# Two PSUM banks in turn, a convolution in six steps and column sums with standing ones, in a kernel of selective scans

## The chip, the cores and the metric

The kernel runs on one core of one Trainium2 chip. The metric is the device time of one execution in microseconds (us). All runs here are of state "fast" (one core, no second state seen). Engines are named as in the profile: PE is TensorE, PEld its weight loads, DVE VectorE, ACT ScalarE, POOL GpSimd, SP the engine that issues the DMAs. `L401` is a line of the kernel; one helper issues most VectorE and GpSimd instructions, so they are told apart by their tiles. A "step" below is a `yield` in a Python generator: the kernel is built by several generators that are advanced in turn, once per scan ("piece"), so a step decides beside which scan an instruction stands in its engine's queue. In the changed kernel's trace all 3198 instructions of VectorE, 5567 of ScalarE and 2255 of GpSimd run in the order of the built program, so an instruction that waits holds up all that stand behind it on its engine.

## The reference, cut to what matters

```python
# per image (4 of them): x is 64 x 64 x 96
xz = bilinear(gn(x), W_in, ...)                    # two halves: xc, z (192 channels each)
t = conv3x3(sign(xc + move0), sign-weights) + conv_b + rp_b0
t = where(t >= 0, t, prelu_a * t) + rp_b1 + xc     # the PReLU
u = silu(t)                                        # written by rows and by columns
# 4 directions: u by rows, by columns, and both reversed
delta = softplus(dts + dt_bias)                    # dts, B, C from a projection of sign(u)
for l in range(4096):                              # the selective scan, 192 channels x 16 states
    h = exp(delta[l] * A) * h + (delta[l] * u[l]) * B[l]
    y[l] = sum over states of h * C[l]
# sum of the 4 directions, layernorm, gate, projection; then attention and a feed-forward layer
```

## The kernel before

It cuts the scans into 1536 pieces of 128 x 1024 (8 channels x 16 states on the partitions). Each piece needs: the decay dA on ScalarE (1.12 us), the input product on GpSimd (2.36 us), the scan on VectorE (2.34 us), the output product on VectorE (1.225 us) or GpSimd (2.35 us), and the sum over states on TensorE. Every eight pieces ScalarE copies the sums `y` out of their PSUM bank, and the delta of a later group is prepared. Everything else (column sums, convolution, projection, epilogue) is "side work", one step per piece.

```python
# the loop, cut
for i in range(n):
    ...
    if i >= 1: self.carry(i - 1)                   # ScalarE, 128x1
    if i % 8 == 3 and i > 8: self.evacuate(i - 4)  # ScalarE copies y out
    if i + 1 < n: self.decay(i + 1)                # ScalarE, dA of the next scan
    if i >= 3: self.reduce(i - 3)                  # TensorE, y in the bank "y"
    if i + AHEAD < n: self.inject(i + AHEAD)       # GpSimd, input product
    self.scan(i)                                   # VectorE
    c.later.tick()                                 # stores that are due
    if i % 8 == 0 and self.todo: lanes.append(self.prepare())
    interleave(lanes); next(back, None)            # one step of delta, one of the side work

# prepare(): delta, its bank is "dps"
<8 matmuls into ps>;                     yield
ACT Abs -> d; ACT Relu -> t;             yield
ACT Exp d; ACT Ln -> ps;                 yield
<TensorE adds t into ps by the identity>; yield
DVE d[:, 1] = ps * u;                    yield     # the product reads ps
ACT d[:, 0] = copy of ps                           # so does the copy

# convolution, for each 96 x 512 part: four steps of 5, 4, 5, 4 taps, and for the part before it
#   step 0: DVE pz = pz*s + v;  DVE pz = r*(1 - a) + pz
#   step 1: ACT sign(pz), ACT Exp    step 2: ACT Ln, Exp    step 3: DVE u = pz*e, ACT turned copy of u
# then a fifth step: ACT v, r from the bank, matmul into pz
```

## Time and profile before

| | before |
|---|---|
| median of the first three runs (5533.6 to 5543.78) | 5537.85 us |
| VectorE busy, of the profiled span of 5538.9 us | 5052.4 us (91%) |
| GpSimd busy | 4994.2 us (90%) |
| ScalarE busy | 3556.7 us (64%) |
| TensorE busy | 3432.7 us (62%) |

The prediction shows the main lines. Three more lines of the list of waits (waiting instruction, what it waited for, total us, times, longest us) turn out to matter:

```profile
ACT ut L614 <- DVE u L401: 91.6, 45, 3.6
...
DVE u L401 <- ACT e L601: 39.8, 16, 2.5
...
ACT pd L1185 <- DVE pd L401: 3.7, 1, 3.7
```

ScalarE's turned copy of u waits 91.6 us for VectorE's u, which stands in the same step. ScalarE's copy of delta (pd), which stands one step behind VectorE's product on the same bank, hardly waits at all: 3.7 us, once. VectorE waits for its inputs of u only in the first convolution, before the scans (16 times).

### The profile page before, as it was taken

What the parts mean: (1) busy time and instruction counts of PE and PEld (TensorE: products, weight loads), DVE (VectorE), ACT (ScalarE), POOL (GpSimd) and SP (SyncE); (2) the same over time, 40 slices, a digit from 0 to 9 for tenths busy, and PEclk for the clock granted to TensorE, in tenths of its full rate; (3) what the DMA queues carried; (4) which work ended last, traced back from release to release, by engine and by line L of the source; (5) the groups of instructions that cost most, each with busy time, mean ns of one, the idle gap of its engine ahead of it and who ended that gap; (6) DMA issues with size and microseconds to landing.
All of it is one profiled execution on the core that took longest, in us unless ns stands there. A gap on an engine that the chain in (4) does not pass through costs nothing. (4 is left out here: it accounts for less than half of the span.)

```text
span 5538.9 us, 62371 instructions
## 1 busy us (share of the span) xinstructions
PE 3432.7 (62%) x20197; PEld 1356.7 (24%) x20197; DVE 5052.4 (91%) x3237; ACT 3556.7 (64%) x5564; POOL 4994.2 (90%) x2262
## 2 busy tenths in 40 slices
PE   6456665576557766577656766544676564444677
PEld 3222222222223222222222222211232121111223
DVE  3299999999999999899999999999999999999984
ACT  4467776777666667677766666755556775555554
POOL 2199999999999999899999999999999999999981
PEclk8667776678767876667777777766787766566778
DMA  4456666866766566666656566665666665665652
GB/s 78 118 179 198 207 194 193 258 193 199 220 203 194 194 205 199 218 217 207 205 193 212 185 200 210 212 211 191 210 215 186 191 205 198 205 208 190 207 159 60
DMA packets 613244, 1069.93 MB, mean 193 GB/s; under 512 B 225083, under 2 KB 343924, under 8 KB 611124
## 3 DMA queue, kind: packets, MB, share of 16 engines
q1 hardware_dynamic: 599428, 1065.88, 61.4%
q8 instruction: 159, 2.61, 0.2%
q10 hardware_dynamic: 13488, 0.07, 0.1%
q14 instruction: 169, 1.38, 0.1%
HBM read 833.20 MB, written 229.38 MB: 192 GB/s over the span
## 5 line engine op out<-in xcount | busy, mean ns | idle before, releaser
L401 POOL TENSOR_TENSOR w<-dl,bc 128x1024 f32<-128x1024 f32 x1536 | 3579.9, 2356 | 166.7 <-PE yp L1302 93.2
L1231 ACT ACTIVATE dA<-dl,anm 128x1024 f32<-128x1024 f32 x1536 | 1715.6, 1117 | 477.0 <-DVE w L401 291.5
L1302 PE MATMUL yp<-w,sum 128*32 128x256 f32 x12288 | 1261.6, 507 | 1083.2 <-ACT ys L1316 621.9
L401 DVE TENSOR_TENSOR_SCAN dA<-dA,cy,w 128x1024 f32<-128x1024 f32 x706 | 1654.4, 2343 | 94.7 <-ACT dA L1231 83.4
L401 POOL TENSOR_TENSOR w<-h,bc 128x1024 f32<-128x1024 f32 x596 | 1402.6, 2353 | 93.7 <-DVE h L401 85.2
L401 DVE TENSOR_TENSOR w<-dA,bc 128x1024 f32<-128x1024 f32 x940 | 1151.4, 1225 | 47.7 <-DVE dA L401 0.5
L401 DVE TENSOR_TENSOR_SCAN h<-dA,cy,w 128x1024 f32<-128x1024 f32 x446 | 1043.3, 2340 | 9.2 <-ACT dA L1231 8.7
L1302 PEld LDWEIGHTS yp<-w,sum 128*32 128x32 f32 x12288 | 308.0, 127 | 2136.9 <-issue 705.4
L1271 ACT COPY cy<-dA 128x1 f32<-128x1 f32 x707 | 110.8, 157 | 692.0 <-DVE w L401 690.7
L401 DVE TENSOR_TENSOR_SCAN dA<-dA,w 128x1024 f32<-128x1024 f32 x234 | 534.2, 2283 | 22.3 <-ACT dA L1231 18.0
L577 PE MATMUL cv<-tp,cw 96*96 96x512 fp8e5 x1152 | 359.9, 456 | 85.6 <-ACT r L627 70.5
L401 DVE TENSOR_TENSOR_SCAN h<-dA,w 128x1024 f32<-128x1024 f32 x150 | 341.8, 2279 | 24.4 <-POOL w L401 23.6
L1179 PE MATMUL dps<-sp,ident 128*128 128x512 f32 x378 | 356.8, 1043 | 0.0
L1307 PE MATMUL yp<-ya,back 128*128 128x256 f32 x576 | 237.8, 534 | 0.0
L577 PEld LDWEIGHTS <-cw 96*96 96x96 fp8e5 x1152 | 159.0, 146 | 277.5 <-issue 223.8
L1271 ACT COPY cy<-h 128x1 f32<-128x1 f32 x445 | 82.7, 186 | 145.6 <-DVE h L401 144.5
L847 PE MATMUL yc<-eys,mean 96*96 96x512 f32 x240 | 134.6, 713 | 33.3 <-DMA eys<-yd 14.5
L1307 PEld LDWEIGHTS yp<-ya,back 128*128 128x128 f32 x576 | 123.9, 248 | 127.8 <-issue 97.1
L1172 ACT ACTIVATE pd<-dps,dbias,pvd 128x512 f32<-128x512 f32 x189 | 143.8, 761 | 16.4 <-PE dps L1167 13.0
L1173 ACT ACTIVATE sp<-dps,dbias,pvd 128x512 f32<-128x512 f32 x189 | 144.7, 766 | 0.0
L401 DVE TENSOR_TENSOR pd<-dps,pu 128x512 f32<-128x512 f32 x189 | 127.6, 675 | 4.6 <-DMA dl<-dld 4.3
L1316 ACT COPY ys<-yp 128x512 f32<-128x512 f32 x192 | 111.7, 582 | 30.2 <-PE yp L1307 24.3
(282 smaller groups left out, 4017.6 us busy)
## 6 DMA issues: line engine op xcount, KB each, us to landing
dl<-dld SPq DMA_DIRECT2D x768, 512.0 KB
bc<-bcd SPq DMA_DIRECT2D x512, 512.0 KB
dld<-pd SPq DMA_DIRECT2D x126, 512.0 KB
yd<-ys SPq DMA_DIRECT2D x768, 64.0 KB
dld<-pd SPq DMA_DIRECT2D x126, 256.0 KB
ya<-yd SPq DMA_DIRECT2D x192, 128.0 KB
pu<-ud SPq DMA_DIRECT2D x32, 512.0 KB
pu<-utd SPq DMA_DIRECT2D x31, 512.0 KB
```

The lines of the kernel that those rows point to most:

```text
L401: return getattr(self.eng, name)(out, *args, **kw)
L577: nc.tensor.matmul(ps, c.cw[:, j, t, 96 * h : 96 * h + 96], tpad[j][:, 8 * q + dy : 8 * q + dy + 8, dx : dx + IW], start=(j == 0 and t == ...
L847: self.c.nc.tensor.matmul(ps, w, x, start=(i == 0), stop=(i == len(pairs) - 1))
L1172: nc.scalar.activation(d[:, 0], ps, AF.Abs, scale=sc, bias=bi)
L1173: nc.scalar.activation(t, ps, AF.Relu, scale=sc, bias=bi)
L1179: nc.tensor.matmul(ps, c.ident, t, start=False, stop=True, skip_group_check=True)
L1231: c.nc.scalar.activation(t, self.dlt[i // NQ][0], AF.Exp, scale=c.anm[:, g, NQ * KORD[e] + q : NQ * KORD[e] + q + 1])
L1271: self.c.nc.scalar.copy(self.carries[g, q], h[:, CH - 1 : CH])
L1302: c.nc.tensor.matmul(y[32 * x : 32 * x + 32, g % 2, :], c.sum4, prod[:, 256 * x : 256 * x + 256], start=(q == 0), stop=(q == NQ - 1 and no ...
L1307: c.nc.tensor.matmul(y[:, g % 2, :], w, src, start=False, stop=(n == len(more) - 1))
L1316: c.nc.scalar.copy(t, y[:, :, ::-1] if k >= 2 else y)
```

## The change

Its intent: TensorE should no longer wait 622 us for the copy of `y` (two banks in turn); VectorE should be relieved of 48 steps of 0.75 us (TensorE adds the relu term in the bank); the side work's steps should be smaller; the column sums should take fewer passes of TensorE.

```diff
-        ps = ... tile(..., tag="dps")              # delta's bank
+        ps = ... tile(..., tag=f"y{1 - self.bank()}")
-            self.ydone[i // 8] = ... tag="y"
+            self.ydone[i // 8] = ... tag=f"y{i // 8 % 2}"
         nc.scalar.activation(d[:, 0], ps, AF.Abs, scale=sc, bias=bi)
+        yield
         nc.scalar.activation(t, ps, AF.Relu, scale=sc, bias=bi)
         yield
         nc.scalar.activation(d[:, 0], d[:, 0], AF.Exp, scale=-1.0)
+        yield
         nc.scalar.activation(ps, d[:, 0], AF.Ln, bias=1.0)
 ...
         c.vec.tensor_tensor(d[:, 1]..., ps..., uv, ALU.mult)
-        yield
         nc.scalar.copy(d[:, 0], ps)
 ...
+            if i + 1 < n:
+                self.decay(i + 1)
             if i % 8 == 3 and i > 8:
                 self.evacuate(i - 4)
-            if i + 1 < n:
-                self.decay(i + 1)
-            if i % 8 == 0 and self.todo:
+            if i % 8 == 4 and self.todo:           # and a fourth delta before the first scan
 # convolution (batches 1 to 3; the first keeps the old steps)
-                for s in range(4):                 # 5, 4, 5, 4 taps
+                for s in range(4 if alone else 5): # 4, 4, 4, 4, 2 taps
+                    if s == 0 and turned:
+                        by_columns(*turned)        # turned copy of the u before, and its store
-                            c.vec.scalar_tensor_tensor(pz, r, c.oma[:, one(ph)], pz, ALU.mult, ALU.add)
+                        elif s == 1 and not alone:
+                            nc.tensor.matmul(pz, c.omad[:, ph], r, start=False, stop=True, ...)
+                        elif s == (3 if alone else 4):
+                            if not alone:
+                                sign(ph, pq, pz)   # before: beside the first Exp
                             u = f32("u" + pn)[0:96]
                             c.vec.tensor_tensor(u, pz, e, ALU.mult)
+            if turned:
+                by_columns(*turned)                # the last one: after the last step
             c.later.flush()
             sub.close()
 # column sums: ones stand, x streams
-            for i in range(NT):
-                nc.tensor.matmul(csum, xts[i // 8][:, i % 8, :], c.ones1, ...)
+            for i in range(0, NT, 4):
+                nc.tensor.matmul(csum, c.ones1, xts[i // 8][:, i % 8 : i % 8 + 4, :]..., ...)
+            # then a copy of the row of 384, four tiny matmuls that turn and add it, a copy
```

(Cut; the scans' carry tiles are also joined, four to a tile.)

More of the change, by code (lines that the diff above doesn't have):

```diff
@@ L137, in hybrid_kernel @@
     acs, acb, oma = ctile("acs", [96, 2]), ctile("acb", [96, 2]), ctile("oma", [96, 2])
+    omad = ctile("omad", [96, 2, 96])
     sbR = ctile("sbR", [128, 2, 2])
@@ L188, in transposed @@
             count[0] += 1
-            ps = p.ps.tile([128, 1024], BF16, name=f"tps{count[0]}", tag=("y", "dps")[count[0] % 2])
+            ps = p.ps.tile([128, 1024], BF16, name=f"tps{count[0]}", tag=f"y{count[0] % 2}")
             at = 0
@@ L277, in weights @@
         nc.vector.tensor_scalar(oma, pv[:, :, PRELU], -1.0, 1.0, ALU.mult, ALU.add)
+        for h in range(2):
+            nc.gpsimd.tensor_scalar(omad[:, h], i96, oma[:, h : h + 1], None, ALU.mult)
         yield
@@ L350, in weights @@
         )
-        ps = p.ps.tile([128, 512], F32, name="tpd", tag="dps")
+        ps = p.ps.tile([128, 512], F32, name="tpd", tag="y0")
         for g in range(3):
@@ L507, in prologue @@
                 yield
-            csum = bank("csum", 0)[0:96, 0:1]
-            for i in range(NT):
-                nc.tensor.matmul(csum, xts[i // 8][:, i % 8, :], c.ones1, start=(i == 0), stop=(i == NT - 1))
-                if i % 8 == 7:
-                    yield
+            csum = bank("csum", 0)[0:1, 0 : 4 * DM]
+            for i in range(0, NT, 4):
+                nc.tensor.matmul(
+                    csum, c.ones1, xts[i // 8][:, i % 8 : i % 8 + 4, :].rearrange("p i e -> p (i e)"),
+                    start=(i == 0), stop=(i == NT - 4),
+                )
+                if i % 8 == 4:
+                    yield
+            row = f32("csr")[0:1, 0 : 4 * DM]
+            nc.scalar.copy(row, csum)
+            ps = bank("cst", 1)[0:96, 0:1]
+            for i in range(4):
+                nc.tensor.matmul(
+                    ps, row[:, DM * i : DM * i + DM], c.ones1[0:1, :], start=(i == 0), stop=(i == 3)
+                )
+            yield
             cs = f32("cs")[0:96, 0:1]
-            nc.scalar.copy(cs, csum)
-            gsum = bank("gsum", 1)[0:96, 0:1]
+            nc.scalar.copy(cs, ps)
+            gsum = bank("gsum", 0)[0:96, 0:1]
             nc.tensor.matmul(gsum, c.grp, cs, start=True, stop=True)
@@ L563, in prologue, with by_columns, sign @@
             one = lambda h: slice(h, h + 1)
-            prev = None
+            prev = turned = None
             two = c.p.dA.tile([128, CH], F32, name=f"cv2_{b}", tag="dA") if alone else None
             utp = sub.enter_context(tc.tile_pool(name=f"ut_{b}", bufs=1))
+            uts = {}
+            def by_columns(h, q, u):
+                if q % 4 == 0:
+                    uts[h] = utp.tile([96, IW, 32], F32, name=f"ut{h}{q}_{b}", tag="ut")
+                ut, at = uts[h], 8 * (q % 4)
+                dst, src = ut[:, :, at : at + 8], u.rearrange("p (h w) -> p w h", w=IW)
+                (nc.gpsimd.tensor_copy if alone else nc.scalar.copy)(dst, src)
+                if q % 4 == 3:
+                    rows = slice(8 * q - 24, 8 * q + 8)
+                    c.later.store(c.utd[b][h].rearrange("p (w h) -> p w h", h=IH)[:, :, rows], ut, after=1)
+            def sign(h, q, pz):
+                sg = f32(f"sg{h}{q}")[0:96, 0:128]
+                nc.scalar.activation(
+                    sg.bitcast(F8).rearrange("p (h e i) -> p h e i", h=8, e=2),
+                    pz.rearrange("p (h i e) -> p h e i", h=8, e=2), AF.Sign, saturate=False,
+                )
+                for m in range(3):
+                    g0 = 64 * (m // 2) + 32 * h
+                    c.later.store(xgw[g0 : g0 + 32, m % 2, 128 * q : 128 * q + 128], sg[m::3, :])
             for n, part in enumerate(parts + [None]):
@@ L572, in prologue @@
                     ps = (two[:, at : at + 512] if alone else bank("cv" + nm, 0))[0:96]
-                for s in range(4):
+                for s in range(4 if alone else 5):
                     if part:
-                        for j, t in taps[(0, 5, 9, 14)[s] : (5, 9, 14, 18)[s]]:
+                        per = 5 if alone else 4
+                        for j, t in taps[per * s : min(18, per * s + per)]:
                             dy, dx = divmod(t, 3)
@@ L581, in prologue @@
                             )
+                    if s == 0 and turned:
+                        by_columns(*turned)
+                        turned = None
                     if prev:
@@ L585, in prologue @@
                             c.vec.scalar_tensor_tensor(pz, pz, pv[:, ph, S_X : S_X + 1], v, ALU.mult, ALU.add)
-                            c.vec.scalar_tensor_tensor(pz, r, c.oma[:, one(ph)], pz, ALU.mult, ALU.add)
-                        elif s == 1:
-                            sg = f32("sg" + pn)[0:96, 0:128]
-                            nc.scalar.activation(
-                                sg.bitcast(F8).rearrange("p (h e i) -> p h e i", h=8, e=2),
-                                pz.rearrange("p (h i e) -> p h e i", h=8, e=2), AF.Sign, saturate=False,
-                            )
-                            for m in range(3):
-                                g0 = 64 * (m // 2) + 32 * ph
-                                c.later.store(xgw[g0 : g0 + 32, m % 2, 128 * pq : 128 * pq + 128], sg[m::3, :])
+                            if alone:
+                                c.vec.scalar_tensor_tensor(pz, r, c.oma[:, one(ph)], pz, ALU.mult, ALU.add)
+                        elif s == 1 and not alone:
+                            nc.tensor.matmul(pz, c.omad[:, ph], r, start=False, stop=True, skip_group_check=True)
+                        elif s == (1 if alone else 2):
+                            if alone:
+                                sign(ph, pq, pz)
                             e = f32("e" + pn)[0:96]
                             nc.scalar.activation(e, pz, AF.Exp, scale=-1.0)
-                        elif s == 2:
+                        elif s == (2 if alone else 3):
                             nc.scalar.activation(e, e, AF.Ln, bias=1.0)
                             nc.scalar.activation(e, e, AF.Exp, scale=-1.0)
-                        else:
+                        elif s == (3 if alone else 4):
+                            if not alone:
+                                sign(ph, pq, pz)
                             u = f32("u" + pn)[0:96]
@@ L605, in prologue @@
                             c.later.store(c.ud[b][ph][:, 512 * pq : 512 * pq + 512], u)
-                            if pq % 4 == 0:
-                                ut = utp.tile([96, IW, 32], F32, name=f"ut{pn}_{b}", tag="ut")
-                            at = 8 * (pq % 4)
-                            dst, src = ut[:, :, at : at + 8], u.rearrange("p (h w) -> p w h", w=IW)
+                            turned = (ph, pq, u)
                             if alone:
-                                nc.gpsimd.tensor_copy(dst, src)
-                            else:
-                                nc.scalar.copy(dst, src)
-                            if pq % 4 == 3:
-                                rows = slice(8 * pq - 24, 8 * pq + 8)
-                                c.later.store(
-                                    c.utd[b][ph].rearrange("p (w h) -> p w h", h=IH)[:, :, rows], ut, after=1
-                                )
+                                by_columns(*turned)
+                                turned = None
                     yield
@@ L633, in prologue @@
                     yield
+            if turned:
+                by_columns(*turned)
             c.later.flush()
@@ L1113, in __init__ @@
         self.bt, self.ct, self.dlt, self.ins, self.dAs, self.carries, self.ydone = {}, {}, {}, {}, {}, {}, {}
-        self.late = None
+        self.late, self.cys = None, {}
         self.us, self.gs, self.at, self.loaded, self.sums = {}, {}, -1, set(), {}
@@ L1119, in done, with bank @@
         return self.at > (b * NK + n) * NPC + SETTLE
+    def bank(self):
+        return max(0, self.at - 3) // 8 % 2
     def load_signs(self, b, k):
@@ L1161, in prepare @@
         d = spare[0] if spare else p.pd.tile([128, 2, 512], F32, name=f"pd_{nm}", tag="pd")
-        ps = spare[3] if spare else p.ps.tile([128, 512], F32, name=f"dps_{nm}", tag="dps")
+        ps = spare[3] if spare else p.ps.tile([128, 512], F32, name=f"dps_{nm}", tag=f"y{1 - self.bank()}")
         pv = ps.rearrange("p (c q s) -> p s q c", q=4, s=8)
@@ L1175, in prepare @@
         nc.scalar.activation(d[:, 0], d[:, 0], AF.Exp, scale=-1.0)
+        yield
         nc.scalar.activation(ps, d[:, 0], AF.Ln, bias=1.0)
@@ L1189, in prepare @@
             then = (lambda: self.loaded.add((b, k, ci, part))) if x == len(groups) - 1 else None
-            c.later.store(dst, d[r0 : r0 + n], after=1, then=then)
+            c.later.store(dst, d[r0 : r0 + n], after=2, then=then)
     def load_bc(self, w, to, b, e, ci, q):
@@ L1246, in scan @@
         if ci < NCH - 1:
-            self.carries[g, q] = c.p.cy.tile([128, 1], F32, name=f"cy_{i}", tag=f"cy{g}{q}")
+            if q == 0:
+                self.cys[g] = c.p.cy.tile([128, NQ], F32, name=f"cy_{i}", tag=f"cy{g}")
+            self.carries[g, q] = self.cys[g][:, q : q + 1]
         lead = c.vec.us - c.gps.us
@@ L1297, in reduce @@
         if i % 8 == 0:
-            self.ydone[i // 8] = c.p.ps.tile([128, 2, 256], F32, name=f"yp_{i}", tag="y")
+            self.ydone[i // 8] = c.p.ps.tile([128, 2, 256], F32, name=f"yp_{i}", tag=f"y{i // 8 % 2}")
         y, prod = self.ydone[i // 8], self.ins.pop(i)
@@ L1324, in run @@
         c, lanes, n = self.c, [], len(self.pieces)
-        w = [c.p.w.tile([128, CH], F32, name=f"w_s{x}", tag="w") for x in range(7)]
+        w = [c.p.w.tile([128, CH], F32, name=f"w_s{x}", tag="w") for x in range(8)]
         ps = [c.p.dA.tile([128, CH], F32, name=f"dA_s{x}", tag="dA") for x in range(2)]
@@ L1345, in run @@
             self.load_dl(m)
+        u = c.p.pu.tile([128, CH], F32, name="pu_s", tag="pu")
+        for _ in self.prepare((w[7].rearrange("p (t l) -> p t l", t=2), w[4][:, 512:CH], u, ps[1][:, 512:CH])):
+            pass
         self.decay(0)
```

## The prediction

> **What bounds the kernel now.** The time before is 5537.85 us. I read the page's busy table first, then the costliest groups, then who waited for whom on VectorE and GpSimd, then the engines' busy time in stretches that I cut at the stages of the side work.
>
> ```profile
> span 5538.9 us, 62371 instructions
> PE 3432.7 (62%) x20197; PEld 1356.7 (24%) x20197; DVE 5052.4 (91%) x3237; ACT 3556.7 (64%) x5564; POOL 4994.2 (90%) x2262
> L401 POOL TENSOR_TENSOR w<-dl,bc 128x1024 f32<-128x1024 f32 x1536 | 3579.9, 2356 | 166.7 <-PE yp L1302 93.2
> L401 POOL TENSOR_TENSOR w<-h,bc 128x1024 f32<-128x1024 f32 x596 | 1402.6, 2353 | 93.7 <-DVE h L401 85.2
> L401 DVE TENSOR_TENSOR w<-dA,bc 128x1024 f32<-128x1024 f32 x940 | 1151.4, 1225 | 47.7 <-DVE dA L401 0.5
> ```
>
> VectorE and GpSimd are both over 90% busy over the whole span. Each of the 1536 scans needs an input product on GpSimd, and afterwards an output product on VectorE (940 of them, 1.225 us) or GpSimd (596, 2.353 us). A counter in the kernel, at build time, deals out the output products, so the two engines form one balanced bound. The stretches (columns: length, then busy us of PE, weight loads, DVE, ACT, POOL; then the TensorE clock) show where they are not full:
>
> ```profile
> 0.00:269.00 269.00, 151.29 (x745) 87.85 (x746) 75.59 (x137) 121.16 (x198) 42.28 (x104) 0.79 0.44 95
> 771.00:961.00 190.00, 109.47 (x888) 48.62 (x886) 181.05 (x104) 127.81 (x195) 182.20 (x80) 0.65 0.61 191
> 1157.00:1429.00 272.00, 186.19 (x1084) 73.61 (x1083) 266.68 (x180) 198.13 (x303) 267.14 (x116) 0.79 0.69 207
> 1638.00:2270.00 632.00, 442.11 (x2320) 162.95 (x2320) 606.39 (x381) 423.81 (x678) 606.07 (x266) 0.73 0.61 196
> 4580.00:4804.00 224.00, 102.22 (x693) 34.21 (x692) 221.22 (x127) 116.93 (x172) 220.45 (x96) 0.61 0.60 195
> 5419.00:5539.00 120.00, 82.76 (x292) 36.68 (x284) 53.42 (x97) 52.31 (x88) 6.95 (x7) 0.79 0.22 62
> ```
>
> First and last are the start (before the first scan) and the end (after the last): 389 us that the change hardly touches. The stretch from 4580 has no side work: 71 scans in 224 us, 3.16 us each, VectorE 98.8% busy. That is the floor. The stretch from 1157 is a convolution: 79 scans, 3.44 us each, yet VectorE is still 98% busy. So a convolution costs time because it gives VectorE **work**, not because it makes it wait. The projection of B and C (from 771) and the epilogue (from 1638) lose 4 to 5% as **waits**.
>
> ```profile
> DVE dA L401 <- ACT dA L1231: 101.3, 86, 5.5
> DVE h L401 <- POOL w L401: 23.6, 2, 14.4
> DVE g L401 <- PE sy L847: 19.7, 9, 4.6
> POOL w L401 <- PE yp L1302: 93.6, 58, 8.6
> POOL w L401 <- DVE h L401: 85.2, 107, 4.1
> PE yp L1302 <- ACT ys L1316: 621.9, 141, 10.8
> ```
>
> (Total us, times, longest.) TensorE waits 622 us for ScalarE's copy of y out of its only bank: the change aims at this. But VectorE waits for GpSimd's products only twice, at the start, while GpSimd waits 85 us for scans. So VectorE leads; TensorE's wait costs time only if it delays GpSimd further than its lead, or holds ScalarE so that the next decay (dA) comes late. I followed each VectorE wait on ScalarE's dA (or its carry copy) over 0.2 us in the loop, some 119 us, back on ScalarE: about 45 us (39 waits near 1.25 us) stand behind a decay that itself waited for VectorE; 27 us behind the epilogue's squares waiting for the yc matmuls; 7 us behind the column sum; 6 us behind turned y still being loaded; and only 4 to 5 us behind the copy of y.
>
> **What the Trainium skill says.** "TensorE: Matmul & The Clock Gate", section "What's actually happening": TensorE drops to half rate after an idle window of about 3.4 us. The trace agrees: eight y matmuls take 1.08 us after a wait of 10 us for the copy and 0.64 us in a busy stretch. Shorter TensorE waits may so speed up what follows. "PSUM — Partial Sum Buffer", section "The four PSUM rules": a matmul without the first-flag adds to what VectorE wrote where the bit stands. Hence the new relu matmul must wait for VectorE's remaining step in that bank; the kernel before already adds the delta's relu term in this way. "DVE: opcode table, instruction layouts, handler registers and perf-mode slots", section "6. Datapath and trigger behaviour": the scan runs at half throughput. The trace agrees (2.34 us against 1.225 us for a product of the same size), so VectorE's main load stays.
>
> **The change, part by part.** I compared the order of instructions of both builds.
> *Relu term on TensorE.* VectorE loses 48 of its 64 scalar-tensor-tensor steps cz<-r,oma,cz (batches 1 to 3; the first keeps its 16) at 751 ns: 36.0 us. The counter then moves 9 output products from GpSimd to VectorE: +9 x 1.225 = 11.0 us. Net VectorE -25.0 us, GpSimd -9 x 2.353 = -21.2 us. Both lie on the bound in stretches 98% busy, so I take the mean: **-23 us**. TensorE gains 48 matmuls of two passes (its f32 counts are twice the instructions), at about 713 ns a pass (the yc row of the same shape): 68 us over three convolutions of some 275 us, where it is 64 to 72% busy. That fits beside the rest.
> *Six steps instead of five.* Four taps a step instead of five, ScalarE's copy of u moved away from u itself. ScalarE's 92 us of waiting for u should vanish, but the convolution's VectorE idles only 5 us in each, so: 0 to -2 us. The side work gets 48 steps longer; in both orders it finishes in time for the fourth direction, without a burst of catch-up.
> *Two banks in turn.* y of one group of eight pieces in one bank, the delta of the next in the other, then swapped. Delta's matmuls begin at piece 4 of a group and ScalarE's last copy of it is issued at piece 10, just before y of the next group wants that bank at piece 11. So TensorE no longer waits for the copy of y, issued at piece 11, but for the copy of delta at piece 10: about one scan (3.4 us) earlier, minus the decay ahead of it. I expect the 622 us to fall to some 300 to 400 us under a new name, not to zero. What of this reaches VectorE: the 4 to 5 us above, with the decay now ahead of the copy of y, and perhaps a fifth of the epilogue's 27 us through a warmer, less late TensorE: **-10 us**.
> *Column sums.* Before: 64 passes a batch, four steps of about 2.7 us. After: 8 matmuls of 384 columns, 16 passes, by the same 713 ns x 384/512 = 535 ns: 8.6 us, four steps of 2.1 us, plus a copy of one row (the 384-wide kvs copy takes 478 ns) and eight tiny passes. In the loop it saves perhaps **-5 us** over three batches; in the first batch the two more hops cost about +2 us.
> *Start.* A fourth delta is prepared before the first scan, in the shadow of the 60 us that GpSimd waits for the first deltas. VectorE must now await its u, queued behind six loads of delta, before the first scan; I estimate 6 to 10 us from their spacing. But it idled 9 us for GpSimd's first product anyway, so **+2 us**. The joined carry tiles only change waits: 0.
> Sum: -23 - 10 - 1 - 5 + 2 + 2 = -35 us, giving about 5503 us. I lean a little further, to 5500 us, for the warmer clock.
>
> **Rivals.** (1) *TensorE was the hidden cause of most idling.* VectorE idles some 160 us in the loop in gaps over 0.2 us. If the copy's stall lies behind half of it, the gain is 23 + 80 = 103 us: 5435 us. For it: 622 us is the largest removable wait, and GpSimd's 94 us follow TensorE. Against: VectorE does not wait for GpSimd, and the chain from each VectorE wait seldom ends at that copy. (2) *The new waits eat the gain.* The relu matmul waits for VectorE inside TensorE's program order, the banks are coupled to ScalarE's delta chain, and GpSimd's wait for free product buffers rises by 20 to 30 us: about 5530 us. For it: TensorE is strictly ordered and already waits 65 us for u before reusing cz's bank. Against: nine product buffers leave TensorE about two scans of slack. (3) *Work alone counts*, every wait is replaced by another: 5515 us.
>
> **Range and chances.** Only the 23 us is firm; the rest is 0 to 80 us by the rivals. Eight in ten: 5455 to 5528 us. Faster by over 2% means below 5427 us, more than even rival 1 gives: 0.06. Slower by over 2% would need a new stall of 110 us: 0.01.
>
> **What would show it.** Right: VectorE busy falls by about 25 us and GpSimd by 21; a convolution takes about 3.3 us a scan and stays 98% busy; TensorE's wait for the copy of y nearly disappears and one for the copy of delta (pd<-dps) takes over a good half of it; VectorE's wait for dA stays above 80 us; the epilogue stretch stays above 3% idle. Wrong: VectorE's wait for dA falls below 50 us (rival 1), or GpSimd's wait for TensorE rises above 110 us (rival 2), or the start or the end, before the first and after the last scan, moves by over 5 us.

## The result, and the profile after

| | before | after |
|---|---|---|
| median of four runs each | 5539.91 us (5533.6 to 5543.78) | 5567.15 us (5560.22 to 5577.43) |
| profiled span | 5538.9 us | 5567.8 us |
| VectorE busy | 5052.4 us | 5029.7 us |
| GpSimd busy | 4994.2 us | 4975.7 us |

The ratio is 1.0052, with a 95% interval of 1.0033 to 1.0071. (A ratio is the mean time of one kernel's fast runs over that of the other's of the same rounds, so not quite the ratio of the medians quoted here. Multiplied with some 5535 us, 0.001 is 5.5 us.) The kernel became 0.5% slower, outside the predicted range, whose upper end was 5528 us.

The page of the changed kernel, its head, busy line and two of the costliest groups (line, engine, operation, tiles, count; then busy us and mean ns; then idle time before it):

```profile
span 5567.8 us, 61980 instructions
...
PE 3556.8 (64%) x20133; PEld 1371.2 (25%) x20133; DVE 5029.7 (90%) x3198; ACT 3546.7 (64%) x5568; POOL 4975.7 (89%) x2255
...
L404 POOL TENSOR_TENSOR w<-h,bc 128x1024 f32<-128x1024 f32 x587 | 1380.5, 2352 | 147.0 <-DVE h L404 138.0
L404 DVE TENSOR_TENSOR w<-dA,bc 128x1024 f32<-128x1024 f32 x949 | 1162.2, 1225 | 55.7 <-DMA bc<-bcd 3.8
```

The work fell as predicted: VectorE by 22.7 us, GpSimd by 18.5 us, nine output products moved to VectorE (940 to 949). So the time did not come from work: over the whole span VectorE is idle 5567.8 - 5029.7 = 538 us, before 5538.9 - 5052.4 = 486.5 us, 51.6 us more. The stretches show in which stages (columns as in the prediction: window, length, busy us of PE, PEld, DVE, ACT, POOL, then clock, DMA share and GB/s; the windows are placed on the same stages, which lie elsewhere in time):

```profile
827.00:1017.00 190.00, 113.70 (x902) 49.13 (x902) 180.67 (x104) 129.42 (x197) 181.15 (x80) 0.67 0.62 195
1217.00:1555.00 338.00, 246.46 (x1297) 95.72 (x1297) 316.65 (x200) 230.11 (x355) 318.25 (x138) 0.75 0.64 200
1762.00:2394.00 632.00, 448.92 (x2302) 163.75 (x2302) 600.19 (x378) 416.41 (x670) 602.97 (x263) 0.72 0.62 200
4600.00:4824.00 224.00, 109.59 (x686) 35.67 (x685) 221.24 (x126) 116.17 (x171) 220.12 (x96) 0.61 0.59 196
5443.70:5567.80 124.10, 87.66 (x288) 39.33 (x277) 53.22 (x97) 52.55 (x88) 6.94 (x7) 0.72 0.21 60
```

The stretch without side work (from 4600) is as before: 71 scans in 224 us, VectorE 98.8% busy. The projection (from 827) is as full as before, 95%; the epilogue (from 1762) lost a little, 95.0% against 95.9%. The convolution (from 1217) is the one that changed: 98 scans, 3.45 us each, as slow as before (3.44), although each scan there carries less work. VectorE's share fell from 98.0% to 316.65 / 338 = 93.7% (8.71 us of it in one wait for gT, see below). The waits say what it waits for:

```profile
ACT pd L1224 <- DVE pd L404: 459.5, 183, 4.1
...
PE yp L1343 <- ACT pd L1224: 327.4, 94, 6.5
...
PE dps L1219 <- ACT dps L1216: 246.8, 98, 7.8
...
DVE dA L404 <- ACT dA L1270: 111.0, 81, 8.7
...
POOL w L404 <- PE yp L1343: 82.6, 51, 8.4
...
DVE u L404 <- ACT sg L597: 11.6, 12, 2.2
...
DVE u L404 <- ACT cy L1312: 9.2, 6, 4.9
```

TensorE's wait for the copy of y (622 us) has gone, and one for the copy of delta has taken half of it (327.4 us), just as predicted. A second wait, not predicted, is new as well: the matmul that adds delta's relu term waits 246.8 us for ScalarE's logarithm. GpSimd waits less for TensorE, not more. But the first line is new: ScalarE waits 459.5 us, in 183 of 188 groups, for VectorE's product of delta, before it copies delta out. And VectorE waits 20.8 us in front of u, for ScalarE's sign and for ScalarE's carry copy ahead of it in the queue (4.9 us of this is one wait that comes from gT, see below).

What the first line does to the bound shows in the order of time (start us, length us, engine, line, operation, tiles; in brackets the idle time before it and what ended it):

```profile
433.61 0.68 DVE L404 TENSOR_TENSOR pd<-dps,pu 128x512 f32<-128x512 f32 x1
434.20 2.34 DVE L404 TENSOR_TENSOR_SCAN h<-dA,cy,w 128x1024 f32<-128x1024 f32 x1
434.32 0.58 ACT L1224 COPY pd<-dps 128x512 f32<-128x512 f32 x1 [2.87 <-DVE pd L404]
...
436.58 1.12 ACT L1270 ACTIVATE dA<-dl,anm 128x1024 f32<-128x1024 f32 x1 [0.29 <-DVE h L404]
...
437.80 2.36 DVE L404 TENSOR_TENSOR_SCAN dA<-dA,cy,w 128x1024 f32<-128x1024 f32 x1 [1.25 <-ACT dA L1270]
```

VectorE's product and ScalarE's copy both read the bank dps. The kernel's framework lets the two engines read one bank only after each other, in the order of the program. So the copy waits 2.87 us until the product has run, which itself stands behind a scan and an output product in VectorE's queue. The next decay dA is queued behind the copy and two activations of the side work (left out above), and it comes 1.25 us after VectorE has run dry. This is less than half of ScalarE's 2.87 us, since ScalarE has 36% slack; but the slack was there to keep dA early. (Up to 0.29 us of the 1.25 is not the copy's: the decay itself still waited for VectorE's scan, see the next paragraph.) All of VectorE's waits for ScalarE over 0.2 us in the loop come to 125.4 us before and 159.9 us after. I followed each back on ScalarE to the nearest wait over 0.15 us (passing over a decay's own wait if under 0.4 us): 22 of them, 23.1 us, stand behind such a copy of delta. In the kernel before there is none. Another rule of following would move such shares by several us.

What the prediction saw and left aside is larger, and it is in every kernel here. Before the change there are 49 places, 54.3 us of VectorE's waiting, where the decay of a piece starts just as the scan of the piece before ends, although ScalarE was idle for 50.6 us of it. Built once more while this was checked, the kernel shows why: decays have two buffers, and to 73 of the 1536 the framework gave the same one as to the piece just before, so the decay must wait for that scan. After the change it is 64 places, with ScalarE idle for 58.1 us. No run here tried to remove this.

The Trainium skill states the rule behind the order: "PSUM — Partial Sum Buffer", section "PSUM bank collisions raise a hardware error", says that two different engines must not access the same bank and group of 32 partitions at the same time, reads included, and that software has to keep them apart. The trace agrees in that in all 187 pairs of product and copy that it names the copy starts at least 0.03 us after the product's end (434.32 against 433.61 + 0.68 = 434.29 above); no run here tried what happens otherwise.

Two more losses stand out, both longer and rarer. At the end of a convolution:

```profile
823.60 6.25 SPq L1236 DMA_DIRECT2D bc<-bcd  x1
...
831.66 0.58 ACT L693 CAST xr<-xa 128x512 bf16<-128x512 f32 x1 [6.55 <-DMA utd<-ut]
...
832.24 1.12 ACT L1270 ACTIVATE dA<-dl,anm 128x1024 f32<-128x1024 f32 x1
...
833.46 2.36 DVE L404 TENSOR_TENSOR_SCAN dA<-dA,cy,w 128x1024 f32<-128x1024 f32 x1 [4.62 <-ACT dA L1270]
```

The last turned u now leaves only after the last step of the convolution, and the projection, whose tile xr takes over the same memory, begins at once. ScalarE waits 6.55 us for that store to land, and VectorE 4.62 us for the dA behind it. The three such places take 17.0 us of VectorE's time, before 5.4 us. And at the first delta of the next batch:

```profile
1469.88 6.08 SPq L1164 DMA_DIRECT2D gT<-gTd  x1
...
1478.20 1.01 PE L1205 MATMUL dps<-gT,wdz 128*128 128x64 fp8e5 x8 [11.00 <-DMA gT<-gTd]
...
1479.25 0.78 ACT L1210 ACTIVATE pd<-dps,dbias,pvd 128x512 f32<-128x512 f32 x1 [8.46 <-PE dps L1205]
...
1482.12 0.59 ACT L638 ACTIVATE e<-cz 96x512 f32<-96x512 f32 x1 [2.10 <-PE cz L632]
...
1483.91 2.36 DVE L404 TENSOR_TENSOR_SCAN dA<-dA,cy,w 128x1024 f32<-128x1024 f32 x1 [8.71 <-ACT dA L1270]
```

The load of the sign matrix gT is issued in the very step that needs it. Its issue took 6.08 us (its neighbours 0.6 us) behind a store of turned u, TensorE waited 11.00 us, ScalarE's Abs waited 8.46 us for TensorE, its next exponential another 2.10 us for the new relu matmul, which TensorE had behind gT's, dA stood behind both, and VectorE idled 8.71 us. TensorE had this wait in the kernel before too (31.1 us in all, now 27.4), but there it reached VectorE with 3.1 us, now with 13.6 us in two places (the second, 4.9 us, stands in front of u). At both ends little moved: the first scan starts at 269.6 us (before 268.96), and the part after the last one is 4 us longer. Single profiles scatter more than that at the ends: conv_only and conv_sign below share their start, and their first scans are at 264.3 and 269.1 us.

### The profile page after: what moved, and what is told of

Same layout as the page of the kernel before. It is cut to its first block, busy times and chain, and to the rows that moved or that the text cites. A ratio compares the mean times of both kernels' runs of the same rounds, so it can differ in the third digit from the quotient of the medians.

```text
span 5567.8 us, 61980 instructions
## 1 busy us (share of the span) xinstructions
PE 3556.8 (64%) x20133; PEld 1371.2 (25%) x20133; DVE 5029.7 (90%) x3198; ACT 3546.7 (64%) x5568; POOL 4975.7 (89%) x2255
## 5 line engine op out<-in xcount | busy, mean ns | idle before, releaser
L1343 PE MATMUL yp<-w,sum 128*32 128x256 f32 x12288 | 1313.9, 523 | 753.9 <-ACT pd L1224 327.4
L404 POOL TENSOR_TENSOR w<-h,bc 128x1024 f32<-128x1024 f32 x587 | 1380.5, 2352 | 147.0 <-DVE h L404 138.0
L404 DVE TENSOR_TENSOR_SCAN h<-dA,cy,w 128x1024 f32<-128x1024 f32 x441 | 1031.8, 2340 | 10.8 <-ACT dA L1270 10.8
L404 DVE TENSOR_TENSOR_SCAN dA<-dA,w 128x1024 f32<-128x1024 f32 x238 | 543.4, 2283 | 28.6 <-ACT dA L1270 23.1
L1219 PE MATMUL dps<-sp,ident 128*128 128x512 f32 x376 | 337.1, 994 | 247.1 <-ACT dps L1216 246.8
L1224 ACT COPY pd<-dps 128x512 f32<-128x512 f32 x188 | 110.0, 585 | 459.5 <-DVE pd L404 459.5
L1348 PE MATMUL yp<-ya,back 128*128 128x256 f32 x576 | 220.1, 499 | 4.8 <-DMA ya<-yd 2.6
L1219 PEld LDWEIGHTS dps<-sp,ident 128*128 128x128 f32 x376 | 82.9, 275 | 376.8 <-ACT dps L1216 332.3
L1205 PE MATMUL dps<-gT,wdz 128*128 128x64 fp8e5 x1000 | 118.7, 321 | 43.2 <-DMA gT<-gTd 27.4
```

What stands on the lines that cost most here:

```text
L404: return getattr(self.eng, name)(out, *args, **kw)
L1205: nc.tensor.matmul(pv[:, s], wd[:, k, s], gT[:, :, c0 : c0 + 16], start=(s == 0), stop=(s == 7))
L1219: nc.tensor.matmul(ps, c.ident, t, start=False, stop=True, skip_group_check=True)
L1224: nc.scalar.copy(d[:, 0], ps)
L1343: c.nc.tensor.matmul(y[32 * x : 32 * x + 32, g % 2, :], c.sum4, prod[:, 256 * x : 256 * x + 256], start=(q == 0), stop=(q == NQ - 1 and no ...
L1348: c.nc.tensor.matmul(y[:, g % 2, :], w, src, start=False, stop=(n == len(more) - 1))
```

## The experiments

My theory after the traces: three orders lose what the work gains, namely (a) the copy of delta in the step of its product, (b) the sign in the step of u, (c) the late store of turned u. The rivals: the two banks, the longer chain or the relu on TensorE cost the time by themselves, or any wait removed comes back under another name. All runs were timed in five rounds against the kernel before, and gave correct results.

| run | ratio to before | 95% interval | median us (before of the same rounds) |
|---|---|---|---|
| conv_only | 1.0032 | 1.0020 to 1.0044 | 5550.49 (5534.19) |
| banks_only | 1.0044 | 1.0032 to 1.0056 | 5555.88 (5534.19) |
| sign_early | 1.0039 | 1.0027 to 1.0051 | 5556.80 (5534.19) |
| copy_late | 0.9990 | 0.9982 to 0.9998 | 5530.37 (5534.19) |
| before_copy_with | 1.0036 | 1.0024 to 1.0049 | 5556.93 (5534.62) |
| merge_only | 1.0109 | 1.0094 to 1.0125 | 5600.11 (5534.62) |
| both_end | 0.9951 | 0.9939 to 0.9964 | 5510.67 (5534.62) |
| full | 0.9924 | 0.9911 to 0.9937 | 5499.23 (5534.62) |
| conv_fixed | 0.9970 | 0.9959 to 0.9981 | 5520.40 (5539.54) |
| banks_fixed | 0.9982 | 0.9975 to 0.9989 | 5528.45 (5539.54) |
| late_split | 0.9982 | 0.9974 to 0.9989 | 5530.19 (5539.54) |
| csum_only | 1.0009 | 1.0003 to 1.0016 | 5543.70 (5539.54) |
| conv_sign | 0.9997 | 0.9989 to 1.0005 | 5535.60 (5536.45) |
| conv_ends | 0.9994 | 0.9986 to 1.0002 | 5533.44 (5536.45) |
| full_old_sums | 0.9904 | 0.9890 to 0.9919 | 5482.64 (5536.45) |

### Each half of the change alone

**conv_only**: the kernel before with the convolution's part of the change (six steps, relu term on TensorE, sign and turned u moved), and the joined carry tiles, without which it does not fit the memory. (These tiles are in both halves; no run takes them alone.)

> The kernel before with only the convolution's part of the change (six steps, relu term on TensorE, sign of the sum next to u, u turned a part later) and the joined carry tiles, without which it does not fit in SBUF. VectorE's work falls by 25 us as in the changed kernel. Theory S (the sign now stands just in front of u on the same bank, so VectorE waits for ScalarE, and the late store of turned u holds the projection's start): the waits eat the 25 us, ratio to before 0.999 to 1.004, VectorE's waits for the sign and for the carry before u about 20 us. Rival B (all of the loss comes from the banks): the convolution keeps its gain, ratio 0.994 to 0.997.

Measured: 1.0032. VectorE busy is 5026.1 us, as much less as in the whole change, and the time still rises. The wait in front of u is there:

```profile
DVE u L404 <- ACT sg L585: 22.4, 12, 8.7
...
2789.98 0.78 ACT L1198 ACTIVATE pd<-dps,dbias,pvd 128x512 f32<-128x512 f32 x1 [8.90 <-PE dps L1193]
...
2791.93 0.69 DVE L404 TENSOR_TENSOR u<-cz,e 96x512 f32<-96x512 f32 x1 [8.65 <-ACT sg L585]
```

(The first line is of the waits, the others of the timeline.) Not all 22.4 us are the sign's own: in the longest of the twelve waits the sign came late because ScalarE's Abs before it waited 8.90 us for the matmuls on gT. The other eleven make 13.8 us.

So this half alone turns 25 us of saved work into a loss of 0.3%.

**banks_only**: the other half: two banks, the steps of delta, the fourth delta before the first scan, the decay ahead of the copy of y, and the joined carry tiles.

> The kernel before with only the banks' part (y and delta in two banks in turn, delta's steps spread, its copy in the same step as its product, fourth delta before the first scan, decay ahead of the copy of y). Theory C (ScalarE's copy of delta stands right behind VectorE's product on the same bank, so ScalarE is held some 2.5 us 180 times and late decays follow): ratio to before 1.004 to 1.008, ScalarE waiting 400 to 480 us for the product of delta. Rival S (the loss is the convolution's): ratio 0.996 to 1.001.

Measured: 1.0044. Its work is that of the kernel before (VectorE 5055.1 us), ScalarE waits 453.9 us for pd, and 16.6 us of VectorE's waits (16 places) stand behind a copy of delta.

### The shared step of product and copy

**copy_late** puts the removed step back; so that the copy doesn't come later than in the changed kernel, Abs and Relu share a step again.

```diff
         nc.scalar.activation(d[:, 0], ps, AF.Abs, scale=sc, bias=bi)
-        yield
         nc.scalar.activation(t, ps, AF.Relu, scale=sc, bias=bi)
 ...
         c.vec.tensor_tensor(d[:, 1]..., ps..., uv, ALU.mult)
+        yield
         nc.scalar.copy(d[:, 0], ps)
```

> The changed kernel with ScalarE's copy of delta one step behind VectorE's product again; Abs and Relu share a step to make room. Theory C: ScalarE's 460 us of waiting for the product fall below 50, the decays come earlier, time falls by 20 to 30 us, ratio to before 1.000 to 1.002. Rival (two banks cost whatever the copy's place, because y must wait for delta): the wait of TensorE for the copy stays near 590 us in both rows and the ratio stays 1.004 to 1.006.

Measured: 0.9990, so about 0.6% below the changed kernel's 1.0052, a little more than theory C said. ScalarE's wait for pd is down to 0.2 us, once.

**before_copy_with** is the reverse: the kernel before, with nothing but this step taken away.

```diff
         c.vec.tensor_tensor(d[:, 1]..., ps..., uv, ALU.mult)
-        yield
         nc.scalar.copy(d[:, 0], ps)
```

> The kernel before with one edit: ScalarE's copy of a finished delta is issued in the same step as VectorE's product that reads the same bank (the step between them is taken away), nothing else. Theory A (the removed step alone costs the time, because ScalarE then waits for VectorE in front of its next decay): ScalarE waits some 400 to 480 us for pd (3.7 us before), VectorE's wait for dA rises by 15 to 30 us, and the time is 1.003 to 1.006 of the kernel before. Theory B (it only hurts together with the two banks in turn, where TensorE needs the bank next): the wait of ScalarE appears, but the time is 0.999 to 1.001.

Measured: 1.0036, for one removed `yield` that changes only the order (VectorE's busy time is 5055.3 us against 5052.4).

```profile
ACT pd L1184 <- DVE pd L401: 406.6, 179, 7.0
...
DVE dA L401 <- ACT dA L1230: 114.2, 103, 3.9
```

ScalarE's wait rose from 3.7 to 406.6 us and VectorE's for dA from 101.3 to 114.2 us; 13 waits of VectorE, 14.8 us, now stand behind a copy of delta. Theory A holds, except that the wait for dA rose by 13 us and not by 15 to 30; B falls: the two banks are not needed for the loss. The shared buffer of two decays is not the reason either: there ScalarE is idle for 51.9 us, before for 50.6.

**merge_only** is the control for copy_late's second edit: Abs and Relu share a step, the copy stays beside the product.

```diff
         nc.scalar.activation(d[:, 0], ps, AF.Abs, scale=sc, bias=bi)
-        yield
         nc.scalar.activation(t, ps, AF.Relu, scale=sc, bias=bi)
```

> The changed kernel with Abs and Relu of a delta in one step again and nothing else; the copy stays in the step of the product. It is the control for copy_late, which did both. Theory A (the copy beside the product is the cause): time 1.003 to 1.006 of the kernel before, ScalarE's wait for pd still over 400 us. Theory B (the longer chain of delta, one step more, is the cause): 0.998 to 1.000, and VectorE's wait for dA at 90 us or less.

Measured: 1.0109, worse than either theory said. Merging is thus not what helped copy_late; product and copy beside each other, now one piece earlier in the group, cost even more. VectorE's waits for ScalarE in the loop are 197.8 us against 159.9 in the changed kernel, so the time is lost there. But those behind copies of delta hardly rose (24.7 us against 23.1); the rest is spread over many causes, such as the sign (11.6 to 19.2 us). Why one piece earlier is so much worse I can't show.

**late_split** puts the step back without merging anything, so the copy comes at the very piece whose y wants the bank.

```diff
         c.vec.tensor_tensor(d[:, 1]..., ps..., uv, ALU.mult)
+        yield
         nc.scalar.copy(d[:, 0], ps)
```

> The changed kernel with only the step between product and copy of delta put back; Abs and Relu stay in steps of their own, so the copy comes one step later than in copy_late, at the piece whose y wants the same bank. Theory A (what matters is that the copy does not stand beside the product): 0.998 to 1.002, ScalarE's wait for pd under 20 us, TensorE's wait for the copy of delta above the 312 us of copy_late (400 to 600). Rival (copy_late was good because its copy came before y wants the bank, a copy any later costs as much as the shared step): 1.004 or more.

Measured: 0.9982.

```profile
PE yp L1344 <- ACT pd L1225: 642.4, 157, 11.7
```

TensorE's wait for the bank has doubled against the changed kernel, to more than the 622 us which the change set out to remove, and the time is 0.7% lower than the changed kernel's. A long wait on TensorE costs nothing here; a shorter one on ScalarE does. Theory A holds, with even more waiting on TensorE than the 400 to 600 us expected.

**banks_fixed** is banks_only with copy_late's edit.

> banks_only (two banks in turn, fourth delta before the first scan, decay ahead of the copy of y) with the copy of delta one step after the product and Abs and Relu in one step. Theory A (the banks themselves are worth next to nothing, because TensorE's wait for the copy of y was not on VectorE's path, and the step shared by product and copy cost all of banks_only's loss): 0.997 to 1.000, ScalarE's wait for pd under 20 us. Rival (the two banks in turn cost time by themselves, by coupling y to delta): 1.002 to 1.005 still. Prediction on record for the banks: about -10 us, 0.998.

Measured: 0.9982, some 10 us gained by this half once the copy stands in a step of its own. Which of its parts gains them (the banks, the decay ahead of the copy of y, the fourth delta) was not run apart; late_split speaks against the shorter wait of TensorE. Its trace no longer has the 5.1 us of VectorE's waits that stand behind the copy of y in the kernel before.

### The sign and the late store

**sign_early**: the changed kernel with the sign where it was.

```diff
-                            if alone:
-                                sign(ph, pq, pz)
+                            sign(ph, pq, pz)
                             e = f32("e" + pn)[0:96]
 ...
-                            if not alone:
-                                sign(ph, pq, pz)
                             u = f32("u" + pn)[0:96]
```

> The changed kernel with the sign back in the step of the first exponential, two steps ahead of u. Theory S: VectorE's waits before u for the sign and the carry (21 us) vanish and the time falls by 15 to 25 us, ratio to before 1.001 to 1.003. Rival C: VectorE's wait only moves to the next decay, ratio stays 1.004 to 1.006.

Measured: 1.0039, only 0.001 below the changed kernel, with overlapping intervals. The wait for the sign has gone, but the one for dA rose from 111.0 to 126.4 us, so little was won: the rival had it right here. (I take it that the copies of delta still stood in ScalarE's way; this run alone doesn't show it.)

**both_end**: copy_late's and sign_early's edits, and two empty steps after the last turned u is stored.

```diff
             if turned:
                 by_columns(*turned)
             c.later.flush()
+            if not alone:
+                yield
+                yield
             sub.close()
```

> The changed kernel with three edits: copy of delta one step after the product (Abs and Relu share a step), sign back in the step of the first Exp, and two empty steps after the last turned u is stored, before the projection reuses its memory. Theory A (these three are where the gain went): VectorE's waits behind xr waiting for the store of turned u fall from 17 to 20 us to under 4, u<-sg to 0, and the time is 0.994 to 0.997. Rival (each wait that is removed comes back under another name): 0.998 to 1.000, as copy_late alone gave 0.999.

Measured: 0.9951, 0.4% below copy_late. The waits of VectorE behind xr and the store of turned u are down to 0.5 us (copy_late 20.5 us), its wait for dA to 74.8 us. Theory A holds.

**conv_fixed**: conv_only with the same two edits (sign, empty steps), without the banks.

> conv_only (the convolution part of the change alone: six steps, relu term on TensorE) with the sign in the step of the first Exp and two empty steps after the last turned u is stored. Theory A (the part saves its 23 to 25 us of work, and lost them to exactly these two orders): u<-sg gone, xr waiting for the store of turned u under 2 us of VectorE's time, 0.994 to 0.997 of the kernel before, against 1.0032 for conv_only. Rival (six steps or the relu on TensorE cost the time by themselves): 0.999 to 1.003.

Measured: 0.9970 against conv_only's 1.0032: what these two edits undo had made a gain of 0.3% into a loss of 0.3%. Theory A holds, at the edge of its range. (VectorE still waits 6.4 and 6.0 us at two of the gT loads in this run.)

**conv_sign** and **conv_ends** take them one at a time.

conv_sign (sign_early's edit on conv_only):

> conv_only with only the sign moved back to the step of the first Exp. Theory A (the sign beside u is the smaller loss: sign_early gave 0.1%): 1.001 to 1.003 of the kernel before, u<-sg gone, and the waits behind xr for the store of turned u stay at about 10 us. Theory B (the sign is the larger loss, 22 us of u<-sg at face value): 0.998 to 1.000.

conv_ends (both_end's two empty steps on conv_only):

> conv_only with only the two empty steps after the last turned u is stored. Theory A (the late store is the larger loss): 0.997 to 0.999 of the kernel before, u<-sg still about 22 us. Theory B (the sign is the larger loss): 1.000 to 1.002.

Measured: 0.9997 and 0.9994. I had expected one to be the larger; the two edits gain the same within the noise, 0.35% and 0.38%, and together 0.62%. The intervals of both include 1, so each alone brings the half back to no change. In conv_sign the waits behind xr stayed (9.5 us, conv_only 8.7), as expected. In conv_ends the wait for the sign fell from 22.4 to 12.1 us, which I had not expected: the one long wait that came from gT no longer stands in front of u. Nor is all of its 0.38%, 21 us, shown to be the late store's. The 8.7 us behind xr are gone, but so are 14.0 us behind the column sum: the two empty steps move every later stage of the side work by two pieces, and no run parts the store from this shift.

### The gT load, and the column sums

**full**: both_end, with gT of the next batch's first direction loaded eight pieces ahead, as the kernel already does for the other directions.

```diff
-        if (ci, part) == (NCH - 1, 0) and k != KORD[-1]:
-            self.load_signs(b, KORD[KORD.index(k) + 1])
+        if (ci, part) == (NCH - 1, 0):
+            at_k = KORD.index(k) + 1
+            nb, nk = (b, KORD[at_k]) if at_k < NK else (b + 1, KORD[0])
+            if (nb, nk % 2) in c.ready:
+                self.load_signs(nb, nk)
```

> both_end with one more edit: the sign matrix gT of the next batch's first direction is loaded eight pieces ahead (as the other directions' already are) and not in the step of the first matmul that needs it. Theory A: TensorE's wait for gT falls from 27 to 36 us to under 8 us, VectorE gains the 14 to 17 us that stood behind it, time 0.992 to 0.995, that is 0.002 to 0.003 below both_end. Rival (the loss is made up by the lead of VectorE's work ahead): within 0.001 of both_end.

Measured: 0.9924. TensorE's wait for gT in the loop has gone (33.8 us in both_end), and the time is another 0.27% lower. The convolution's stretch is full now, 328.70 / 338 = 97.2% of VectorE in the window from 1217, which in the changed kernel held one of the waits for gT and was at 93.7%.

**csum_only**: the kernel before with the column sums' part of the change's diff alone.

> The kernel before with only the column sums by standing ones. Prediction on record: -5 us in the loop, +2 before the first scan, 0.9995. Theory A: VectorE's waits behind the column sum (7 us in the kernel before) go to under 3 us, the time is 0.998 to 1.000. Rival (its extra hops and shifted stages cost as much): 1.000 to 1.003.

Measured: 1.0009, a small loss where I had predicted a small gain. TensorE's busy time fell by 10 us, and VectorE's waits behind the column sum fell from 6.6 to 0.3 us; but those behind the epilogue's squares rose from 21.3 to 27.4 us. (The profiled run was the slowest of its 21, so I rest nothing on its other differences.)

**full_old_sums**: full with that part of the diff reversed.

> The best kernel so far (full) with the column sums of the kernel before. Theory A (the new column sums cost 5 us wherever they stand, as csum_only measured): 0.9905 to 0.992, that is 0.001 below full (0.9924). Theory B (the 5 us were a shift of later stages, and here the old sums bring back the 7 to 14 us of waits behind the column sum): 0.993 to 0.996.

Measured: 0.9904, 5482.64 us, the best kernel of this study: 1.5% below the changed kernel (1.0052 - 0.9904) and 54 us below the kernel before by the medians.

```profile
span 5479.1 us, 62407 instructions
...
PE 3561.9 (65%) x20293; PEld 1397.9 (26%) x20293; DVE 5021.6 (92%) x3198; ACT 3552.5 (65%) x5564; POOL 4972.7 (91%) x2255
...
DVE dA L404 <- ACT dA L1261: 76.7, 64, 5.8
```

(The first two lines are of the page, the third of the waits.) The new column sums cost 0.1 to 0.2% in both places, with intervals of full and full_old_sums that overlap. In full the first scan starts 4.2 us later than in full_old_sums (273.4 against 269.1 us), which is within the scatter of single profiles; csum_only shows no such shift, so where its own 5 us lie stays open.

## Why the prediction was wrong, point by point

- **The bound and the work.** Right. VectorE's busy time fell by 22.7 us (predicted 25.0), GpSimd's by 18.5 us (21.2), the relu matmuls took 67.9 us on TensorE (68) and hardly reached VectorE's waits, but for the 2.10 us at the gT load. The gain is to be had: conv_fixed measured -0.30%, that is -17 us, against the -23 and -1 of the sum.
- **The step that failed.** "Delta's matmuls begin at piece 4 of a group and ScalarE's last copy of it is issued at piece 10": true, but VectorE's product was issued at piece 10 as well, since the change takes away the step between them. I had read the copy's place only from the side of TensorE, which waits for it, and not asked what the copy itself would wait for. In place of "-10 us" this part measured +0.44% alone (banks_only), some 24 us of loss; the removed step by itself makes 0.36% (before_copy_with), 20 us.
- **"Six steps instead of five: 0 to -2 us."** Failed as well. I saw that ScalarE's 92 us of waiting for u would vanish (it did; what that is worth was not run apart), and missed two new orders in the same lines: the sign now reads the bank in front of u (0.35%), and the last turned u is stored where the projection is about to take its memory (0.38%, the shift of the later stages included). Undoing both gave 34 us, which is more than the saved work.
- **The waits of TensorE.** The name and size were right (predicted 300 to 400 us, measured 327.4), and rival 1 was rightly refused: late_split waits 642 us and is faster. The new 246.8 us of waiting for ScalarE's logarithm were missed. banks_fixed did gain the 10 us. Of the mechanisms I gave for them, the decay ahead of the copy of y agrees with its trace (5.1 us), while a warmer TensorE doesn't: the mean granted clock is 0.703 there, 0.708 in the changed kernel and 0.714 in the kernel before. So that the size came out is partly luck. (The two speeds of the y matmuls are in the trace before the change: after a wait of over 3.4 us, 144 of 150 groups of eight took about 1.08 us. But so did 455 of 1179 groups with no wait in front.)
- **Column sums.** Predicted -5 and +2 us, measured +5 us (csum_only); a mis-sized term whose cause stays open.
- **Start.** +2 us predicted, 0.6 us measured, both within the scatter of single profiles; within it VectorE waited 18.3 us for its u, not the 6 to 10 us estimated, but this replaced the wait for GpSimd's first product.
- **gT.** Not in the sum at all. TensorE's wait of 31 us was in the profile before; I took it for hidden, and there it was (3.1 us reached VectorE). In the changed kernel 13.6 us reach it, in conv_only, where delta starts at its old piece, 7.7 us and the 8.65 us in front of u: so it takes no new bank to bring it out, only other neighbours.
- **The rivals.** Rival 2 ("the new waits eat the gain", 5530 us) was nearest, but GpSimd's wait for TensorE, which it named, fell from 93.6 to 82.6 us. The new waits that cost were on ScalarE, ahead of dA. Of the signs in "What would show it", only the convolution's failed (3.45 us a scan and 93.7% busy, instead of 3.3 and 98%). The one on dA stood at 111.0 us and was read as right, since it only watched for a fall.
- **The floor.** "A decay that itself waited for VectorE" (39 waits, 45 us) was read from the trace and not followed up. It is the shared buffer described above, and it outlives every edit: full_old_sums still has 48 such places, 54.8 us.

The sum of -35 us, giving 5503 us, describes the kernel that I believed I was reading. full, which is the changed kernel with these orders mended, measured 5499.23 us. That the two agree so closely is partly luck: it contains -15 us of gT that I had not counted, and the column sums' +5.

## What to carry to other kernels

When a change moves or removes a step in a software-built schedule, list for every engine which two instructions become neighbours, and whether they touch one bank: an engine that only reads may wait for another that only reads. What a wait costs is decided by what stands behind it in the same queue: here 642 us of waiting on TensorE were free, while ScalarE's 407 to 460 us in front of the decay cost 0.4 to 0.6%. A store whose source memory is reused, and a load that is issued where it is needed, should be placed some pieces early; these two edits, the earlier sign and the restored step, with the old column sums, made a slowdown of 0.5% into a gain of 1.0%. And an edit that inserts steps moves everything behind it: compare the waits of the later stages too before the gain is put down to the place that was edited.

## What the Trainium skill lacked or had wrong

- "PSUM — Partial Sum Buffer", section "PSUM bank collisions raise a hardware error", gives the rule that two engines' accesses to one bank must be kept apart, reads included, but not what keeping them apart can cost: here one step less between VectorE's product and ScalarE's copy of the same bank made ScalarE wait 406.6 us instead of 3.7 us, and the kernel 0.36% slower.
- "DMA: Bandwidth & Descriptors", section "Latency and other measured facts", gives about 600 ns to the first byte for a DMA whose descriptors are made in hardware. The issues behind the store of turned u took 6.08 and 6.25 us in the queue of SP where their neighbours took 0.6 us; the section has no figure for such an issue. In the changed kernel exactly 16 of the 3765 issues took over 5 us (5.64 to 8.35), and they are those right behind the 16 stores of turned u; what makes them long was not tested.
